# Expert 0's input rows are loaded and transposed inside the attention, into the memory of the low-rank projections

## The chip, the cores and the metric

The kernel runs on one core of a Trainium2 chip, as one launch. The metric is the device time of one execution in microseconds (us), median of several runs. Engines are named as in the profile: PE (TensorE, its weight loads as PEld), DVE (VectorE), ACT (ScalarE), POOL (GpSimd) and SP (SyncE, which only issues DMAs here).

## The reference

Two transformer blocks on 2 x 2048 tokens of width 256 in float32. Each adds an attention and a feed-forward of the same layernormed input to the residual.

```
x = L0_attn_x
xn = _layernorm(x, axis=-1)
x = x + _L0_attn_ref(xn, ...) + _L0_ffn_ref(xn, L0_ffn_Wg, L0_ffn_W_in, L0_ffn_W_out)
xn = _layernorm(x, axis=-1)
x = x + _L1_attn_ref(xn, L1_attn_key_param, ...) + _L1_ffn_ref(xn, ...)
return x
```

- Block 0's attention is causal with low-rank projections: `q = x @ Wqa @ Wqb` (rank 64), `kv = x @ Wkva @ Wkvb` (rank 32), 16 query heads of width 16 on 4 key heads, rotary embedding, softmax, output projection.
- Block 0's feed-forward is a mixture of 8 experts: each token goes to its two best experts, each expert has places for 1280 tokens, and computes `gelu(a) * g` from its 256 x 1024 input weights and then a 512 x 256 output product. The results are weighted with the gates and added.
- Block 1's attention is against 32 fixed pattern keys, with a sparsemax in place of the softmax. Its weights do not depend on the tokens, so that they can be folded together ahead (`Wq` with the keys, `Wv` with the keys).
- Block 1's feed-forward is a mixture of 8 experts with sigmoid scores, and a shared expert.

## The kernel before, in words

The kernel has three stages: block 0's attention (with the routing of its experts inside), block 0's experts, and block 1.

**Stage 1, attention (L274 to L1171).** Low-rank projections of all tokens are kept in `low` (L285, filled at L374). From it come queries and keys by the products of L385 to L390 and L432 to L436, through DRAM (`qd`, `kd`) back into the tiles `q` and `ks`. The 32 work items j (batch, block of 512 queries, group of heads) are handled in a fixed order. For each there are two passes: `maxima` (L454; scores `s` and their row maxima on DVE, L471), whose result is flipped on PE (`mtT`, L485), copied by DVE into `mr` (L490) and written into two rows of the query tile by DMA (`place_max`, L492), and then `score` (L500; scores `sc` on PE, exponentials `es` on ACT at L510, a mask on POOL at L512) and `values` (L515; `av` on PE). When four items of a block are done, `normalize` (L526) transposes `av` on DVE and `project` (L550) multiplies with the output weights into `po`, DVE adds it to `xo` (L556), and SP stores `xo` into `x1` (L558).

Meanwhile the routing is computed, and POOL scatters the normalised token rows, each with its target and gate (258 words), to the experts' places in the DRAM array `buf` (`dispatch`, L656, 64 indirect DMAs). Expert 0's weights are loaded late in this stage into `cs_sb` (`wi0`, `wt0`; L272, L1169), whose rotary tables are no longer needed by then.

The order of instructions in this stage is written by a loop (L1153) with a cost model: `T` holds a model time of each engine, `candidates()` (L1093) offers the next steps on PE with the time at which each could start, and the best one is written. Steps on other engines and DMAs are put into `jobs` by `later` and written by `flush` (L691) when the model says that they are ready. Instructions written by `pin` keep this order on their engine.

PSUM is shared in this stage by `ps2` (2 tiles of two banks: maxima, flips, projections), `pssc` (3 banks: scores) and `psav` (1 bank: `av`).

**Stage 2, experts (L1215 to L1308).** The memory of stage 1 is given back and given out again. Here the order on each engine is the scheduler's, which follows the program's data and its own estimates. ACT issues ten loads of block 1's weights that are to be folded (L1215 to L1228). Then, for each expert: SP loads its 1152 rows from `buf` (`load_rows`, L1236; 1161 KB), DVE takes targets and gates out of them (`places`, L1241), PE transposes the rows in 18 steps of 128x128, ACT and DVE copying the result into `inT` (`transposed`, L1248). Then come three blocks of 384 rows (`feed_forward`, L1260): for each of four parts, two products `pa` and two `pg` (L1267; each of 128 rows against 384 columns), a Gelu on ACT (L1269) and a product on DVE into `hT` (L1270); then three times four products `py` (L1274), a scaling by the gates on DVE into `ys` (L1277) and a scatter with addition to `x1` by POOL (L1279). Rows and weights of later experts are loaded by SP ahead, into two buffers each. A branch at L1300 handles experts with more than 1152 tokens.

**Stage 3, block 1 (L1310 on).** The weights are folded (L1352 to L1384), and the rest is written by a list scheduler (`Plan`, L49), whose instructions all carry line L138.

Of the kernel before, what the change touches and what calls it, by code (L numbers as in the profile page):

```python
# [145 lines left out]
def moe_transformer_kernel(  # L146
# [121 lines left out]
    cctx = ctx.enter_context(ExitStack())  # L268
    csp = cctx.enter_context(tc.tile_pool(name="csp", bufs=1, side="right"))
    cs_sb = csp.tile([P, 2, S], F32, name="cs_sb")  # L270

    wi0 = cs_sb[:, 0].rearrange("p (c f) -> p c f", c=2)  # L272
    wt0 = cs_sb[:, 1, 0:4 * E].rearrange("p (c e) -> p c e", c=4)
    with ExitStack() as actx:  # L274
# [7 lines left out]
        ps2 = actx.enter_context(tc.tile_pool(name="ps2", bufs=2, space=PSUM))  # L282
        pssc = actx.enter_context(tc.tile_pool(name="pssc", bufs=3, space=PSUM))
        psav = actx.enter_context(tc.tile_pool(name="psav", bufs=1, space=PSUM))
        low = attw.tile([96 + NE, NT], F32, name="low")  # L285
        wq16 = attw.tile([64, 2, 16, 16], F32, name="wq16")
        wkv16 = attw.tile([96, 12, 16], F32, name="wkv16")
        wout_sb = attw.tile([P, 2, E], F32, name="wout_sb")
# [80 lines left out]
        def lows(grp):  # L369

            ps = ps2.tile([P, 512], F32, tag="ps2", name="lw")
            for dc in range(2):
                mm(ps[:96 + NE], lhsT=wa_sb[:, dc], rhs=st[grp]["xnT"][:, dc], start=dc == 0, stop=dc == 1)
            pin(A.copy(low[:, 512 * grp:512 * grp + 512], ps[:96 + NE]))  # L374

        def logits(grp):
            tp = ps2.tile([P, 4, NE], F32, tag="ps2", name="tpl")
# [278 lines left out]
        def dispatch(ti, k):  # L656
# [2 lines left out]
            pin(G.indirect_dma_start(ways[(2 * ti + k) % 4], bass.IndirectOffsetOnAxis(ap=idx_sb[:, k, ti:ti + 1], axis=0),  # L659
                                     xss[ti], None, bounds_check=NSLOT - 1, oob_is_err=False))  # L660

# [428 lines left out]
        def candidates():  # L1093
            now = T["PE"]
            sw = lambda mode: SWITCH * (mode != model["mode"])
            if pos["sc"] < len(scs):
                t = scores_at(now)
                yield t - now + sw("sc") - (150 if T["A"] < now + 300 else 0), t, do_scores
            if pos["av"] < len(avq):
                j, c = avq[pos["av"]]  # L1100
                t = max(now, when("es", j, c, 0), when("es", j, c, 1), at.get("av", 0) if c == 0 else 0,
                        when("v", j // 16, c // 4))
                if c == nch(j) - 1 and j % 4 == 1 and at.get("atts", 0) == 2:
                    t = INF
                yield t - now + sw("av"), t, do_values
            if flips:
                t = max(now, when("neg", flips[0]), free2[-2])
                yield t - now + sw("f") - 400, t, do_flip
            if pos["u"] < len(units):
                j, i, kb = units[pos["u"]]  # L1110
                slack = (main_at[j] - model["scores"]) - (unit_end[j] - model["maxima"]) - LEAD
                t = max(now, when("q", j), when("k", j // 16, kb), free2[-2])
                t2 = max(t, free2[-1] - 230)
                late = -600 if slack < 1 else 0 if slack < MOST else 900
                yield t2 - now + sw("s") + late, t, do_maxima
            for k, (due, ready, dur, f) in enumerate(prep[:1]):
                t = max(now, ready(), free2[-2] if dur else 0)
                late = -500 if due - model["maxima"] < 2 else -100 if due - model["maxima"] < 9 else 2500
                yield t - now + late, t, lambda k=k: prep.pop(k)[3]()
            if projects:  # L1120
                bq, i0, ready = projects[0]
                t = max(now, ready, when("xo", bq), free2[-2])
                late = -300 if now > ready + 15000 else 100

                def go():
                    if i0:
                        projects.pop(0)
                    else:
                        projects[0][1] = 2
                    p_project(bq, i0)  # L1130
                yield t - now + late, t, go
# [18 lines left out]
        for i in range(NSLOT // 512):  # L1150
            later("S", ISSUE, 50000 + 12000 * i, lambda i=i: clear(buf, i), None, 2)
            later("S", ISSUE, 340000 + 40000 * i, lambda i=i: clear(buf1, i), None, 2)
        while pos["av"] < len(avq) or jobs or projects or scat["ti"] < NTILE:  # L1153
            prefetch()
            refetches()
            keys_back()
            scatter()
            flush()
            cand = [z for z in candidates() if z[1] < INF]

            events = [job[4] for job in jobs if job[4] > T["PE"]] + [T["S"], T["V"], T["G"], T["A"]]
            events = [t for t in events if t > T["PE"]]
            best = min(cand, key=lambda z: z[:2]) if cand else None
            if best and best[1] <= min(events + [INF]) + 400:
                best[2]()
            else:
                t1 = min(events) if events else T["PE"] + 500
                T["PE"] = t1
            if not prep and not at.get("w0") and pos["u"] > len(units) - 20:  # L1169
                at["w0"] = 1  # L1170
                later("S", 2 * ISSUE, T["PE"], lambda: load_expert(0, wi0, wt0), None, 2)  # L1171

    x_sb = ctx.enter_context(tc.tile_pool(name="xp", bufs=1)).tile([P, NTILE, E], F32, name="x_sb")
    l1w = ctx.enter_context(tc.tile_pool(name="l1w", bufs=1))
# [37 lines left out]
            v = v.rearrange("p (a b c) -> p a b c", a=shape[1], b=shape[2])  # L1212
        return v

    sq = {}  # L1215
    for nm, ap in (("wqT", wqT), ("wk", wk), ("wv", wv)):
        sq[nm] = fold_tile(P, 2, E)
        A.dma_start(sq[nm], ap.rearrange("(c p) m -> p c m", p=P))
    kp_sb = fold_tile(P, 2, NPAT)
    A.dma_start(kp_sb, kpT.rearrange("(c p) m -> p c m", p=P))  # L1220
    bqk = fold_tile(P, 2, 2)
    A.dma_start(bqk, bqk2)
    bv_sb = fold_tile(1, E)
    A.dma_start(bv_sb, bv)
    A.dma_start(wo_sb, wo.rearrange("(c p) m -> p c m", p=P))
    A.dma_start(bo_sb, bo.broadcast_to([P, E]))
    A.dma_start(gw_sb, gw.rearrange("(c p) m -> p c m", p=P))
    A.dma_start(lb_sb, lb)  # L1228


    with tc.tile_pool(name="moe", bufs=2) as mp, tc.tile_pool(name="moeh", bufs=3) as hp, \
            tc.tile_pool(name="moetp", bufs=2, space=PSUM) as mtp, \
            tc.tile_pool(name="moeps", bufs=2, space=PSUM) as mps:
        tiles = CAP0 // P

        def load_rows(e):  # L1236
            rows = mp.tile([P, tiles, ROW], F32, tag="rows", name="rows")
            SP.dma_start(rows, buf[CAP * e:CAP * e + CAP0].rearrange("(c p) d -> p c d", p=P))
            return rows

# [19 lines left out]
        def feed_forward(wi, wt, inT, n, to, gates_e, c0, x1s):  # L1260
            hT = mp.tile([P, 4, STEP], F32, tag="hT", name="hT")
            for f in range(4):
                pa = mps.tile([P, 512], F32, tag="pa", name="pa")
                pg = mps.tile([P, 512], F32, tag="pg", name="pg")
                for ps, col in ((pa, P * f), (pg, FF + P * f)):
                    for dc in range(2):
                        PE.matmul(ps[:, :n], lhsT=wi[:, dc, col:col + P], rhs=inT[:, dc], start=dc == 0, stop=dc == 1)  # L1267
                ge = hp.tile([P, STEP], F32, tag="ge", name="ge")
                A.activation(ge[:, :n], pa[:, :n], AF.Gelu)  # L1269
                V.tensor_tensor(hT[:, f, :n], ge[:, :n], pg[:, :n], ALU.mult)  # L1270
            for i in range(n // P):
                py = mps.tile([P, E], F32, tag="py", name="py")
                for f in range(4):
                    PE.matmul(py, lhsT=hT[:, f, P * i:P * i + P], rhs=wt[:, f], start=f == 0, stop=f == 3)  # L1274
                c = c0 + i
                ys = hp.tile([P, E], F32, tag="ys", bufs=6, name="ys")
                V.tensor_scalar(ys, py, gates_e[:, c:c + 1], None, ALU.mult)  # L1277

                G.indirect_dma_start(x1s[c % len(x1s)], bass.IndirectOffsetOnAxis(ap=to[:, c:c + 1], axis=0), ys, None,  # L1279
                                     compute_op=ALU.add)  # L1280

        STEP = 384
        last = bass_types.dram_disjoint_views(x1[:], 3)
        rows = load_rows(0)
        for e in range(NE):
            wi, wt = experts[e]
            to, gates_e = places(rows, tiles)
            inT = mp.tile([P, 2, CAP0], F32, tag="inT", name="inT")
            transposed(rows, tiles, inT)
            if e + 1 < NE:  # L1290
                rows = load_rows(e + 1)
            for c in range(2):
                SP.dma_start(wall[P * e:P * e + P, P * c:P * c + P], fg[:, c, e])
                SP.dma_start(wall[P * e:P * e + P, E + P * c:E + P * c + P], fu[:, c, e])
            SP.dma_start(wall[P * e:P * e + P, 2 * E:3 * E], fd[:, e])
            for s0 in range(0, CAP0, STEP):
                feed_forward(wi, wt, inT[:, :, s0:s0 + STEP], STEP, to, gates_e, s0 // P, last if e == NE - 1 else [x1[:]])
            if e + 2 < NE:
                experts.append(next_expert(e + 2))
        with tc.If(tc.nc.values_load(longer[0:1, 0:1], min_val=0, max_val=1) > 0):  # L1300
# [753 lines left out]
```

## Time and profile before

| what | value |
|---|---|
| runs: median, lowest, highest | 2124.32, 2123.40, 2124.34 us |
| the profiled execution's own time | 2125.51 us |
| its span, first to last instruction | 2123.8 us |
| mean granted TensorE clock | 0.952 of full speed |
| stage 1 ends on PE (last `po`) | about 1201 us |
| stage 2 ends on PE (last `py`) | about 1605 us |
| expert 0, PE, from first `tp` to expert 1's first `tp` | 1209.3 to 1262.4 us |
| DMA, mean | 89 GB/s |

Times in the profile are microseconds from the first instruction. A timeline row has the start, the length, the engine, the line, the operation, the tile written and the tiles read, shapes and a count; in brackets stands how long the engine was idle before, and what ended that wait. One matrix product in float32 makes two rows of PE where it needs two passes of weights, so that two products of `pa` appear as x4. The granted clock is the share of TensorE's full speed that the chip's throttle allowed in a stretch. A line such as L310 or L138 is that of a helper that writes many kinds of instruction: there the names of the tiles tell them apart.

### The profile page before, as it was taken

The page shows a single profiled execution, that of the slowest core. Times are in us where ns is not written, and L with a number is a line of the kernel's source. Part 1 is how long each engine was busy: PE and PEld are TensorE (multiplying, and loading weights), DVE is VectorE, ACT ScalarE, POOL GpSimd, SP SyncE. Part 2 cuts the span into 40 slices and gives each one's busy share as a digit, 9 for nine tenths or more (in the row PEclk, how much of TensorE's full clock was granted, in tenths as well). Part 3 has the DMA queues.
Part 4 walks back from the last instruction along what each step waited for, and adds up shares of the span by engine and source line. Part 5 has one row for each costly group of instructions (what it writes and reads, how often), then busy time and mean ns, then how long its engine had stood idle before and what let it go on. Part 6 is the DMA issues. An engine that isn't in the chain of part 4 may idle for free. (4 is left out here: it accounts for less than half of the span.)

```text
span 2123.8 us, 26286 instructions
## 1 busy us (share of the span) xinstructions
PE 1927.7 (91%) x9525; PEld 1070.7 (50%) x9534; DVE 1386.4 (65%) x1943; ACT 913.7 (43%) x1834; POOL 721.2 (34%) x914
## 2 busy tenths in 40 slices
PE   4689999899999999999999799999998998878886
PEld 2344443444444444444443366666765755666664
DVE  4576688676787578778784122222226599999896
ACT  3044456355555655665567411111112333554452
POOL 5232211443444333431101022222230088466551
PEclk8599899899999999999999899999999799999999
DMA  5433321242132322321200333333223022444417
GB/s 148 127 118 103 101 71 38 82 130 67 59 101 84 100 91 64 92 85 32 91 11 11 123 82 75 77 77 77 52 28 105 11 80 88 134 146 145 154 59 238
DMA packets 141384, 188.98 MB, mean 89 GB/s; under 512 B 15678, under 2 KB 109252, under 8 KB 141251
## 3 DMA queue, kind: packets, MB, share of 16 engines
q1 hardware_dynamic: 114672, 135.03, 21.1%
q0 software_dynamic: 23552, 50.46, 9.4%
q10 hardware_dynamic: 3026, 1.77, 0.3%
q8 instruction: 77, 1.26, 0.2%
q14 instruction: 57, 0.46, 0.1%
HBM read 100.74 MB, written 90.66 MB: 90 GB/s over the span
## 5 line engine op out<-in xcount | busy, mean ns | idle before, releaser
L510 ACT ACTIVATE es<-sc 128x512 f32<-128x512 f32 (+3 forms) x1280 | 599.6, 536 | 457.7 <-PE sc L310 447.0
L471 DVE TENSOR_REDUCE part<-s 128x2 f32<-128x1024 f32 (+3 forms) x640 | 650.4, 1059 | 210.5 <-PE s L310 209.3
L310 PE MATMUL sc<-q,ks 128*128 128x512 f32 (+3 forms) x1280 | 425.5, 418 | 19.5 <-ACT es L510 18.9
L310 PEld LDWEIGHTS sc<-q,ks 128*128 128x128 f32 x1280 | 211.7, 191 | 249.0 <-ACT es L510 174.5
L310 PE MATMUL av<-es,va 128*32 128x512 f32 (+3 forms) x2560 | 303.2, 552 | 3.4 <-POOL es L512 1.8
L512 POOL TENSOR_SCALAR_AFFINE_SELECT es<-es 128x256 f32<-128x256 f32 x256 | 103.4, 407 | 561.5 <-ACT es L510 560.5
L310 PE MATMUL s<-ks,q 64*128 64x512 f32 (+3 forms) x1280 | 253.1, 447 | 33.8 <-DVE part L471 11.2
L138 DVE TENSOR_TENSOR srt<-srt 128x1024 f32<-128x1024 f32 (+3 forms) x224 | 224.0, 1036 | 7.6 <-ACT to L138 0.5
L310 PEld LDWEIGHTS s<-ks,q 64*128 64x128 f32 x1280 | 111.6, 189 | 200.6 <-DVE part L471 110.5
L1279 POOL DMA_INDIRECT x<-ys,to x72 | 111.5, 1549 | 294.6 <-DVE ys L1277 165.5
L1270 DVE TENSOR_TENSOR hT<-ge,pg 128x384 f32<-128x384 f32 x96 | 53.2, 554 | 178.1 <-PE pg L1267 176.9
L1269 ACT ACTIVATE ge<-pa 128x384 f32<-128x384 f32 x96 | 47.1, 490 | 269.4 <-PE pa L1267 269.4
L138 POOL DMA_INDIRECT oe<-xn,to x80 | 109.3, 1367 | 76.0 <-ACT xn L138 56.2
L1267 PE MATMUL pa<-inT,wi 128*128 128x384 f32 x336 | 123.3, 486 | 0.0
L1267 PE MATMUL pg<-inT,wi 128*128 128x384 f32 x336 | 122.1, 486 | 0.0
L138 POOL DMA_INDIRECT buf<-xn,slot x64 | 87.7, 1371 | 99.9 <-DVE rc L138 80.7
L1274 PE MATMUL py<-wt,hT 128*128 128x256 f32 x504 | 112.2, 379 | 0.0
L138 ACT COPY srt<-srt 128x1024 f32<-128x1024 f32 (+2 forms) x80 | 67.2, 840 | 101.6 <-DVE srt L138 89.4
L310 PEld LDWEIGHTS av<-es,va 128*32 128x32 f32 x2560 | 55.7, 109 | 100.5 <-issue 76.3
L1274 PEld LDWEIGHTS py<-wt,hT 128*128 128x128 f32 x504 | 95.8, 190 | 17.5
L1277 DVE TENSOR_SCALAR ys<-py,gates 128x256 f32<-128x256 f32 x72 | 34.8, 484 | 86.0 <-PE py L1274 86.0
L1267 PEld LDWEIGHTS pg<-inT,wi 128*128 128x128 f32 x336 | 63.3, 190 | 42.7
(265 smaller groups left out, 2308.2 us busy)
## 6 DMA issues: line engine op xcount, KB each, us to landing
q<-qd SPq DMA_DIRECT2D x64, 256.0 KB
buf<-zero SPq DMA_DIRECT2D x20, 516.0 KB
buf<-zero SPq DMA_DIRECT2D x20, 514.0 KB
xn<-buf SPq DMA_DIRECT2D x20, 514.0 KB
rows<-buf SPq DMA_DIRECT2D x8, 1161.0 KB
qd<-hi SPq DMA_DIRECT2D x16, 512.0 KB
qd<-lo SPq DMA_DIRECT2D x16, 512.0 KB
xn<-oe SPq DMA_DIRECT2D x16, 512.0 KB
```

The lines of the kernel that those rows point to most:

```text
L138: return lambda *a, **k: self.tc.keep_in_program_order(f(*a, **k))
L310: pin(PE.matmul(*args, **kw))
L471: pin(V.tensor_reduce(parts[j][:, i, 2 * pair:2 * pair + 2, kb], sc[:, :, :n], AX.X, ALU.max))
L510: pin(A.activation(es[:, g % 2, :n], sc[:, :n], AF.Exp, scale=0.25))
L512: pin(G.affine_select(es[:, :, 0:P], es[:, :, 0:P], pattern=[[0, 2], [1, P]], compare_op=ALU.is_ge, fill=0.0, base=0, channel_multiplier=-1))
L1267: PE.matmul(ps[:, :n], lhsT=wi[:, dc, col:col + P], rhs=inT[:, dc], start=dc == 0, stop=dc == 1)
L1269: A.activation(ge[:, :n], pa[:, :n], AF.Gelu)
L1270: V.tensor_tensor(hT[:, f, :n], ge[:, :n], pg[:, :n], ALU.mult)
L1274: PE.matmul(py, lhsT=hT[:, f, P * i:P * i + P], rhs=wt[:, f], start=f == 0, stop=f == 3)
L1277: V.tensor_scalar(ys, py, gates_e[:, c:c + 1], None, ALU.mult)
L1279: G.indirect_dma_start(x1s[c % len(x1s)], bass.IndirectOffsetOnAxis(ap=to[:, c:c + 1], axis=0), ys, None, compute_op=ALU.add)
```

## The change

- `low` is allocated in the pool beside `cs_sb`, on 128 partitions, so that it outlives the attention. Its memory, when the projections are no longer needed, holds expert 0's rows (`rows0`) and two of three parts of its transposed rows (`inT0`); the third lies in the free half of `cs_sb`.
- When expert 0's weights have been asked for and all scatters are written, SP gets three loads of 384 rows each (`load_rows0`).
- When all maxima are written, the loop may write `turn_rows0`: six transposes on PE into one `ps2` tile and one copy of 128x768 on DVE, three times.
- In stage 2, expert 0 uses these; `rows` of even experts live in `rows0`, those of odd experts in one other buffer, where there were two.
- `py` gets a PSUM pool of its own, ahead of that of `pa` and `pg`. So `pa` and `pg` lie where the attention's `pssc` and `psav` were, and `py` where a part of `ps2` was.
- The ten loads of weights to be folded are issued by SP in the program's text of expert 1, not by ACT ahead of stage 2.

```
@@
-        low = attw.tile([96 + NE, NT], F32, name="low")
+    low = csp.tile([P, NT], F32, name="low")
+
+    rows0 = low[:, 0:CAP0 // P * ROW].rearrange("p (c d) -> p c d", d=ROW)
+    inT0 = [low[:, CAP0 // P * ROW + 768 * i:CAP0 // P * ROW + 768 * i + 768] for i in range(2)] + [cs_sb[:, 1, 4 * E:4 * E + 768]]
+    inT0 = [v.rearrange("p (c n) -> p c n", c=2) for v in inT0]
@@
+        def load_rows0(i):
+            sdma(rows0[:, 3 * i:3 * i + 3], buf[384 * i:384 * i + 384].rearrange("(c p) d -> p c d", p=P))
+
+        def turn_rows0(i):
+
+            tp = ps2.tile([P, 2, 512], F32, tag="ps2", name="tp0")
+            for dc in range(2):
+                for c in range(3):
+                    flip(tp[:, dc, P * c:P * c + P], rows0[:, 3 * i + c, P * dc:P * dc + P], ident)
+            pin(V.tensor_copy(inT0[i], tp[:, :, 0:384]))
@@ candidates()
+            if pos["u"] == len(units) and at.get("turned", 0) < 3:
+                i = at.get("turned", 0)
+                t = max(now, when("row0", i), free2[-2])
+
+                def turn():
+                    at["turned"] = i + 1
+                    t = use2(1500, "t", 0, lambda: turn_rows0(i))
+                    free2.append(on("V", 1000, t))
+                yield t - now + 200, t, turn
@@ the loop
+            if at.get("w0") and scat["ti"] == NTILE and not at.get("r0"):
+                at["r0"] = 1
+                for i in range(3):
+                    later("S", ISSUE, T["PE"] + 8000, lambda i=i: load_rows0(i),
+                          lambda t, i=i: at.update({("row0", i): t}), 2)
@@ stage 2
-        A.dma_start(sq[nm], ap.rearrange("(c p) m -> p c m", p=P))
...
+    def load_fold():
+        for v, ap in ((sq["wqT"], wqT), (sq["wk"], wk), (sq["wv"], wv), (kp_sb, kpT), (wo_sb, wo), (gw_sb, gw)):
+            SP.dma_start(v, ap.rearrange("(c p) m -> p c m", p=P))
+        SP.dma_start(bqk, bqk2)
+        SP.dma_start(bv_sb, bv)
+        SP.dma_start(bo_sb, bo.broadcast_to([P, E]))
+        SP.dma_start(lb_sb, lb)
@@
+            tc.tile_pool(name="moepy", bufs=2, space=PSUM) as mpy, \
             tc.tile_pool(name="moeps", bufs=2, space=PSUM) as mps:
@@
+        rows_of = [rows0, mp.tile([P, tiles, ROW], F32, tag="rows", bufs=1, name="rows")]
+
         def load_rows(e):
-            rows = mp.tile([P, tiles, ROW], F32, tag="rows", name="rows")
+            rows = rows_of[e % 2]
@@
-                py = mps.tile([P, E], F32, tag="py", name="py")
+                py = mpy.tile([P, E], F32, tag="py", name="py")
@@
-        rows = load_rows(0)
+        rows = rows0
...
             to, gates_e = places(rows, tiles)
-            inT = mp.tile([P, 2, CAP0], F32, tag="inT", name="inT")
-            transposed(rows, tiles, inT)
+            if e == 0:
+                parts_in = inT0
+            else:
+                inT = mp.tile([P, 2, CAP0], F32, tag="inT", name="inT")
+                transposed(rows, tiles, inT)
+                parts_in = [inT[:, :, s0:s0 + STEP] for s0 in range(0, CAP0, STEP)]
             if e + 1 < NE:
                 rows = load_rows(e + 1)
+            if e == 1:
+                load_fold()
```

More of the change, by code (lines that the diff above doesn't have):

```diff
@@ L373, in lows @@
                 mm(ps[:96 + NE], lhsT=wa_sb[:, dc], rhs=st[grp]["xnT"][:, dc], start=dc == 0, stop=dc == 1)
-            pin(A.copy(low[:, 512 * grp:512 * grp + 512], ps[:96 + NE]))
+            pin(A.copy(low[:96 + NE, 512 * grp:512 * grp + 512], ps[:96 + NE]))
         def logits(grp):
@@ L1152, in moe_transformer_kernel @@
             later("S", ISSUE, 340000 + 40000 * i, lambda i=i: clear(buf1, i), None, 2)
-        while pos["av"] < len(avq) or jobs or projects or scat["ti"] < NTILE:
+        while pos["av"] < len(avq) or jobs or projects or scat["ti"] < NTILE or at.get("turned", 0) < 3:
             prefetch()
@@ L1213, in fold_tile @@
         return v
-    sq = {}
-    for nm, ap in (("wqT", wqT), ("wk", wk), ("wv", wv)):
-        sq[nm] = fold_tile(P, 2, E)
-        A.dma_start(sq[nm], ap.rearrange("(c p) m -> p c m", p=P))
[L1219 to L1228, printed above, removed]
+    sq = {nm: fold_tile(P, 2, E) for nm in ("wqT", "wk", "wv")}
+    kp_sb, bqk, bv_sb = fold_tile(P, 2, NPAT), fold_tile(P, 2, 2), fold_tile(1, E)
+    def load_fold():
[5 more added lines that the diff above has]
+        SP.dma_start(lb_sb, lb)
     with tc.tile_pool(name="moe", bufs=2) as mp, tc.tile_pool(name="moeh", bufs=3) as hp, \
             tc.tile_pool(name="moetp", bufs=2, space=PSUM) as mtp, \
+            tc.tile_pool(name="moepy", bufs=2, space=PSUM) as mpy, \
             tc.tile_pool(name="moeps", bufs=2, space=PSUM) as mps:
         tiles = CAP0 // P
+        rows_of = [rows0, mp.tile([P, tiles, ROW], F32, tag="rows", bufs=1, name="rows")]
         def load_rows(e):
-            rows = mp.tile([P, tiles, ROW], F32, tag="rows", name="rows")
+            rows = rows_of[e % 2]
             SP.dma_start(rows, buf[CAP * e:CAP * e + CAP0].rearrange("(c p) d -> p c d", p=P))
@@ L1296, in moe_transformer_kernel @@
             for s0 in range(0, CAP0, STEP):
-                feed_forward(wi, wt, inT[:, :, s0:s0 + STEP], STEP, to, gates_e, s0 // P, last if e == NE - 1 else [x1[:]])
+                feed_forward(wi, wt, parts_in[s0 // STEP], STEP, to, gates_e, s0 // P, last if e == NE - 1 else [x1[:]])
             if e + 2 < NE:
```

## The prediction

> **What bounds the kernel now.** First the page's busy line and its slices: TensorE (PE) is busy nine tenths of the span, so a change gains where PE stands still or runs slowly.
>
> ```profile
> PE 1927.7 (91%) x9525; PEld 1070.7 (50%) x9534; DVE 1386.4 (65%) x1943; ACT 913.7 (43%) x1834; POOL 721.2 (34%) x914
> ...
> PE   4689999899999999999999799999998998878886
> ...
> PEclk8599899899999999999999899999999799999999
> ```
>
> Slice 23 (1168 to 1221 us) shows a 7 among nines. It is where the attention ends and the experts begin, the place that the change touches. The timeline of PE there:
>
> ```profile
> 1193.31 0.70 PE L310 MATMUL po<-wout_sb,att 128*128 128x256 f32 x2
> 1196.04 4.98 PE L310 MATMUL po<-wout_sb,att 128*128 128x256 f32 x14 [2.03 <-DVE att L541]
> 1209.30 1.94 PE L1254 MATMUL tp<-ident,rows 128*128 128x128 f32 x8 [8.29 <-DMA rows<-buf]
> ...
> 1231.36 1.45 PE L1267 MATMUL pa<-inT,cs_sb 128*128 128x384 f32 x4
> ...
> 1241.68 5.34 PE L1274 MATMUL py<-cs_sb,hT 128*128 128x256 f32 x24
> ...
> 1246.86 1.45 PE L1267 MATMUL pa<-inT,cs_sb 128*128 128x384 f32 x4
> ...
> 1262.36 1.04 PE L1254 MATMUL tp<-ident,rows 128*128 128x128 f32 x8
> ```
>
> PE ends the last projection (po) at 1201.02, waits 8.29 us for expert 0's rows, and only then transposes them. One block of 384 rows costs 15.5 us when nothing is missing (1231.36 to 1246.86); the first block takes from 1209.30 to 1231.36, 22.06 us. The table of stages gives the reason for much of that (columns: stretch, its length, busy us of PE, PEld, DVE, ACT, POOL with counts, granted clock, DMA share, GB/s):
>
> ```profile
> 1190.00:1193.00 3.00, 2.55 (x27) 1.23 (x24) 0.00 (x0) 1.91 (x8) 1.58 (x4) 1.00 0.00 0
> 1193.00:1196.00 3.00, 1.01 (x6) 0.41 (x6) 1.68 (x3) 0.00 (x0) 0.62 (x1) 1.00 0.00 0
> 1196.00:1198.50 2.50, 2.46 (x8) 2.08 (x9) 0.41 (x1) 0.00 (x0) 0.00 (x0) 0.70 0.00 0
> 1198.50:1201.00 2.50, 2.50 (x7) 1.64 (x6) 0.28 (x1) 0.00 (x0) 0.00 (x0) 0.62 0.00 0
> ...
> 1205.00:1209.00 4.00, 0.00 (x0) 0.00 (x0) 0.00 (x0) 0.00 (x0) 0.00 (x0) 0.50 1.04 331
> ...
> 1214.00:1216.00 2.00, 2.00 (x6) 0.98 (x5) 0.69 (x1) 0.27 (x1) 0.00 (x0) 0.50 1.07 354
> ...
> 1218.00:1222.00 4.00, 4.00 (x14) 2.29 (x13) 1.11 (x2) 1.14 (x3) 0.00 (x0) 1.00 1.05 391
> ```
>
> The granted clock is halved from about 1197, recovers briefly, and is 0.50 again until about 1217. From 1222 to the last expert PE is busy over 99% of each stretch at clock 1.00, so what is gained here arrives at the end of the experts, and what follows (chain of waits: sorts on DVE, projections) starts from there.
>
> **The change, part by part.**
>
> *Removed wait.* Expert 0's rows no longer load after the attention: 8.28 us (1201.02 to 1209.30). What is late next is the Gelu: its table load and first call wait for the last po, 1.28 + 0.49 us by the timeline, while PE has 3.9 us of products to do before it needs that buffer. So nothing shows there.
>
> *Removed serial transposes and slow clock.* First block 22.06 minus 15.50 = 6.56 us. The rest of expert 0, two blocks, is unchanged.
>
> *Moved product.* In the changed program's order, the first pa (2 products, 1.29 us by 1.29 us from one pa to the next pg in a full block) stands behind the first po. It waits only for the transpose of av on DVE, which ends at 1194.25, and po resumes at 1196.04: it fits. Gain 1.3 us.
>
> *Clock.* The seven remaining po products take 4.98 us at the lowered clock; at the 0.43 us that a py of the same width takes (5.2 us for 12) they would take 3.0 to 3.1. PE was busy a third of 1193 to 1196; with pa there it is about three quarters. TensorE: Matmul & The Clock Gate, Part 1, of the Trainium skill says that the clock is halved after an idle window of about 3.4 us and restored after a busy one. The trace halves it after a hole of only 2.03 us beside thin work, so a window need not be empty. By the page's wording the clock stays up once the hole is filled (gain 1.9); by the trace alone a fall is still possible (gain 0). I take 1.9, since 90% busy stretches just before hold 1.00, and keep 0 for the range.
>
> *Added in the attention: 18 transposes on PE, 3 copies on DVE.* They stand beside the last flip of maxima and in the next 7 us.
>
> ```profile
> 1146.28 0.60 PE L313 MATMUL mtT<-ident,mt 128*8 128x128 f32 x4 [0.54 <-DVE mt L483]
> ...
> 1147.62 1.34 SPq L316 DMA_DIRECT2D q<-mr  x2
> ...
> 1154.81 0.50 PE L310 MATMUL sc<-q,ks 128*128 128x512 f32 x1 [0.16 <-ACT es L510]
> ```
>
> Eight transposes take 1.04 us in the row of 1262.36, 0.13 each, so 18 cost 2.3 us. The same page, Part 4, speaks against the change: about 275 ns for one transpose in a kernel. The records here show 273 ns too, but they overlap; by the page's figure 18 would be 5.0 us. I take the row. Six stand where PE waited 0.54 us; the other twelve stand among diagonal scores, where PE waits 0.16 to 0.34 us for the exponentials. Cost 1.5 us, bounds 0.5 and 3. The DVE copies (128x768; a 128x512 one takes 0.68, so 1.0 us each by size) find DVE idle for 8.13 us, but the first is ahead of the copy of mr, which feeds the loads of the last maxima: these leave about 0.7 us later. They are issued at 1147.62 to 1148.96, and the scores that need them start at 1154.81, so over 2 us of cover remain with a landing of some 3 us; without it, 0.7 us.
>
> *Row loads, moved past SP's queue.* Three loads stand between the last q loads and the next mr loads:
>
> ```profile
> 941.07 2.57 SPq L316 DMA_DIRECT2D q<-qd  x4
> 960.04 1.45 SPq L316 DMA_DIRECT2D q<-mr  x2
> ```
>
> The first waits for the last scatter, which POOL issues at 947.23 (one lands about 5 us after the issue before it). So SP is held until about 952.5; behind it stands only the 960.04 load. 1161 KB at 331 to 400 GB/s take 3.5 us, done by 957. Cost zero; without that idle time up to 8 us of late maxima. PE needs the data at 1146.
>
> *Fold loads, moved from ACT's queue to SP's.* ACT loses ten issues that held nothing else. On SP they stand behind rows of experts 1 and 2 and the weights of experts 1 and 2. DMA: Bandwidth & Descriptors (Issuing engines are not separate DMA queues) says that the same 16 engines serve all issuers, so the bytes cost the same; the order does not. DVE, in order, now meets three waits on loads inside expert 0: rows 1 and rows 2 (for their slots), and bqk. All of these are late relative to the po end, 1200.6 in my sum. Rows 1, x1's store and rows 2 are 2834 KB: at 350 GB/s landed about 10 us after po. The first ys is due 11 us after it. bqk has about 7.1 MB up to it: 20.4 us plus 2 of latency gives 1223, and its issue waits for expert 2's weights to land, so up to 1226. DVE reaches that copy at 1223.1, with hT behind it that PE needs at 1226.4. I take 0.5 us for all these waits, bounds 0 and 3. Expert 1's weights (before bqk in the queue) are needed only at 1246. The buffers that moved in SBUF and PSUM add no instruction; I count zero.
>
> **The sum.** 8.28 + 6.56 + 1.3 = 16.1 (the same from the other side: 61.3 us from the po end to expert 1's first tp become three blocks of 15.5 less 1.3, 45.2); plus 1.9 for the clock, minus 1.5 and 0.5: 16.0 us. The profiled execution took 2125.51 us around its span of 2123.8, so 2109.5 for such a one; the median of the runs is 1.19 below it: 2124.32 - 16.0 = 2108.3.
>
> **The rivals.**
> *The sum without the clock, or with a dearer insertion (0.28).* The clock falls at the hole as before (+1.9), the insertion costs 3 (+1.5) or bqk arrives late (+2.5): 2109.8 to 2114.2, likeliest 2112. For it: the gate already fell in a stretch that was a third busy; against: the hole is filled.
> *Hidden anyway (0.04).* The experts' scatter-adds, not PE, set the end. On POOL's timeline they follow 4.5 us apart (1228.87, 1233.33); 72 of them are 324 us, from the first one (about 1214) to 1538, against 1600 for PE. It would give 2122 to 2126, with the gain left as idle PE at the end. Little speaks for it.
> *Slower (0.05).* DVE's queue in expert 0: bqk's copy blocks hT, and PE with it, until the load lands. Each us past 1226.4 costs one. The gain is eaten at 1242, and the time is slower by over 0.2% past 1247, which means 7.1 MB in 46 us, 155 GB/s. At 140 it would land at 1253, 27 us late: 2124.3 - 16.0 + 27 = 2135. The stretches above show 331 to 391.
> *The change does not do what it says* is left at almost nothing: in its order the row loads, transposes and copies do stand in the attention.
>
> **How the numbers follow.** My forecast 0.63 (2106.8 to 2109.8), the rivals 0.28, 0.04 and 0.05. The range runs from all bounds good (insertion 0.5, no waits: 2106.8) to the second case's end, 2114.2, and 0.9 us further at both ends, which is how far the three runs of before lie apart: 2105.9 to 2115.1. A measurement here tells about 0.2% (4.2 us) from no change: faster 0.91, same 0.04, slower 0.05.
>
> **What would show it.** In the new profile: no wait of PE for rows at the attention's end; the first pa inside the 2 us hole; granted clock near 1.00 from 1190 on; the first tp of expert 1 at about 1246; three row loads near 952 to 957; DVE's copy of bqk without a long wait; from expert 1 on, the same 48 us an expert. I am wrong if PE waits in expert 0 for hT or py for more than 3 us, if the last scores start over 2 us later, or if the experts' gain is lost before the end.

## The result, and the profile after

| | before | after |
|---|---|---|
| median of the runs, us | 2124.33 (2123.4 to 2124.51, 4 runs) | 2107.21 (2105.72 to 2109.07, 4 runs) |
| ratio to before | | 0.9914, 95% interval 0.9902 to 0.9927 |
| profiled execution, us | 2125.51 | 2105.72 |
| its span, us | 2123.8 | 2103.9 |

The change takes 17.1 us off the median; the interval of the ratio reaches from 15.5 to 20.8 us. The kernel was measured twice more beside the experiments, with ratios of 0.992 (0.9907 to 0.9934) and 0.9916 (0.9891 to 0.9941). The prediction was 16.0 us, a median of 2108.3 us.

The page of after, the rows of busy time, of PE's slices and of the granted clock:

```profile
PE 1922.6 (91%) x9534; PEld 1069.6 (51%) x9534; DVE 1387.5 (66%) x1943; ACT 912.4 (43%) x1831; POOL 716.0 (34%) x914
...
PE   4688999899999999999999999999998999888886
...
PEclk8599999899999999999999999999998799999999
```

The 7 and the 8 in the slice where the attention hands over to the experts (PE and clock) have become nines. PE's busy time is 5 us less, on as many matmuls (9534 records, 9525 before): the same work, less of it at a lowered clock. The timeline of PE over the same place:

```profile
1190.04 0.70 PE L313 MATMUL po<-wout_sb,att 128*128 128x256 f32 x2
1191.03 1.56 PE L1294 MATMUL pa<-low,cs_sb 128*128 128x384 f32 x4 [0.29 <-DVE t L536]
1192.77 3.29 PE L313 MATMUL po<-wout_sb,att 128*128 128x256 f32 x14 [0.18 <-DVE att L544]
1195.89 1.46 PE L1294 MATMUL pg<-low,cs_sb 128*128 128x384 f32 x4
...
1241.14 1.04 PE L1281 MATMUL tp<-ident,rows 128*128 128x128 f32 x8
...
1242.91 0.81 PE L1294 MATMUL pa<-inT,wi 128*128 128x384 f32 x2
```

Three things are to be seen. The wait of 8.29 us for rows is gone, and so are the transposes behind it: pg follows po at once. The first pa stands between the two po. From the start of the first po to that of the second it is 2.73 us, to the hundredth what it was before (1193.31 to 1196.04), so the product cost nothing there. And the seven po behind the hole (the 2 us between the two po) take 3.29 us, where they took 4.98. ACT starts its table load for the Gelu right behind the last po:

```profile
1196.13 1.28 ACT L1296 ACT_TABLE_LOAD   x1 [7.01 <-PE po L313]
```

The stages (stretch, its length, busy us of PE, PEld, DVE, ACT and POOL, granted clock, DMA share, GB/s):

```profile
1190.00:1193.00 3.00, 2.53 (x10) 1.21 (x8) 1.68 (x3) 0.00 (x0) 0.62 (x1) 1.00 0.00 0
1193.00:1196.00 3.00, 3.00 (x15) 2.64 (x15) 0.69 (x1) 0.00 (x0) 0.00 (x0) 1.00 0.00 0
1196.00:1200.00 4.00, 4.00 (x14) 2.35 (x13) 1.49 (x4) 2.27 (x3) 0.40 (x2) 1.00 0.71 188
1200.00:1210.00 10.00, 10.00 (x40) 7.30 (x39) 2.96 (x9) 0.98 (x2) 1.63 (x1) 1.00 1.05 362
```

PE is full from 1193 on at a granted clock of 1.00. The loads of the other experts' rows and weights keep the DMA engines as busy as before (1.05), now beneath PE's work.

**Where the time came from.** A single execution wanders by several us, so the stretch is measured between marks next to the change. M is the issue of the last but one pair of `q<-mr` loads of the attention (the expectations below call it the last maxima loads; the very last pair, at 1147.62 before, follows 45.3 us later, in after 45.7), P the first of the last po products, X the first pa of expert 1.

| us | M | M to P | M to X | span |
|---|---|---|---|---|
| before | 1102.36 | 90.95 | 161.76 | 2123.8 |
| after | 1098.47 | 91.57 | 144.44 | 2103.9 |
| after, second profile (c1_after) | 1094.94 | 91.55 | 144.43 | 2101.2 |
| after, third profile (c2_after) | 1099.67 | 91.61 | 144.47 | 2105.2 |
| e2_fold_only | 1098.69 | 90.93 | 158.76 | 2119.1 |
| e3_late_turn | 1096.64 | 91.02 | 150.45 | 2109.9 |
| e4_psum_back | 1103.30 | 91.61 | 148.51 | 2113.3 |
| e5_double_turn | 1094.97 | 93.47 | 146.34 | 2102.3 |
| e6_fill_hole | 1100.87 | 91.58 | 146.78 | 2110.6 |

From M to X the change gains 17.3 us. It divides into -0.62 up to P, 1.69 in the po (4.98 to 3.29), and 16.25 from po's end to X (1201.02 to 1264.12 before; 1196.06 to 1242.91 after). The three profiles of after agree within 0.04 us there, while M itself lies anywhere in 4.7 us. The profiled spans differ by 19.9 us: 3.9 of that had arisen before M, and after the experts 1.3 is lost again, which one profile of before can't put down to the change. Nor can the 3.9 be: e2_fold_only, with the attention of before, has M at 1098.69, and e4_psum_back, with that of after, at 1103.30.

### The profile page after: what moved, and what is told of

The parts are those of the page before. It is cut to its first block, busy times and chain, and to the rows that moved or that the text cites. A ratio compares the mean times of both kernels' runs of the same rounds, so it can differ in the third digit from the quotient of the medians.

```text
span 2103.9 us, 26294 instructions
## 1 busy us (share of the span) xinstructions
PE 1922.6 (91%) x9534; PEld 1069.6 (51%) x9534; DVE 1387.5 (66%) x1943; ACT 912.4 (43%) x1831; POOL 716.0 (34%) x914
## 5 line engine op out<-in xcount | busy, mean ns | idle before, releaser
L138 POOL DMA_INDIRECT buf<-xn,slot x64 | 83.1, 1299 | 100.8 <-DVE rc L138 81.6
```

Source lines behind the costliest of these rows:

```text
L138: return lambda *a, **k: self.tc.keep_in_program_order(f(*a, **k))
```

## The experiments

Each ratio is to the kernel before, measured beside the run. The median of before was 2126.32 us beside e1 to e4, 2124.79 beside e5, e6 and c1_after, and 2125.74 beside e7, e8 and c2_after, so ratios compare better than medians do.

**The fold loads put back on ACT (e1_fold_act).** Expert 0's rows stay in the attention; the ten loads are issued by ACT ahead of expert 0, as before.

```
     def load_fold():
-            SP.dma_start(v, ap.rearrange("(c p) m -> p c m", p=P))
+            A.dma_start(v, ap.rearrange("(c p) m -> p c m", p=P))
...
+    load_fold()
...
-            if e == 1:
-                load_fold()
```

> The changed kernel with its ten fold loads issued by ACT ahead of the experts, as before the change. My theory (the gain is expert 0's removed wait, its transposes and the clock; moving the fold loads is needed because ACT's queue would hold the Gelu): in the profile of before the ten issues took ACT from 1201 to 1211, so the first Gelu comes about 10 us after the last po in place of 1.5, PE stands about 8 us in expert 0, and the time is about 8 us above the changed kernel (some 2115). Rival (where the fold loads are issued does not matter, only the bytes do): within 1 us of the changed kernel, no PE wait in expert 0.

Measured: 2118.6 us, ratio 0.9961 (0.9948 to 0.9973): by the ratios some 9 to 10 us slower than after (8 were expected). The timeline of ACT and PE in this kernel (lines of other engines left out):

```profile
1198.58 0.46 ACTq L1248 DMA_DIRECT2D xn<-in_wqT_dram  x1
...
1201.45 0.48 ACTq L1248 DMA_DIRECT2D gw_sb<-in_gw_dram  x1
1204.03 0.35 ACTq L1249 DMA_DIRECT2D xn<-in_bqk_dram  x1
1207.42 0.49 ACTq L1250 DMA_DIRECT2D xn<-in_bv_dram  x1
1207.54 1.94 PE L1282 MATMUL tp<-ident,rows 128*128 128x128 f32 x8 [5.12 <-DMA rows<-buf]
...
1208.36 0.74 ACTq L1252 DMA_DIRECT2D lb_sb<-in_lb_dram  x1
1209.49 1.28 ACT L1297 ACT_TABLE_LOAD   x1 [17.89 <-PE tp L1282]
1210.79 0.87 ACT L1297 ACTIVATE ge<-pa 128x384 f32<-128x384 f32 x2
...
1211.33 2.93 PE L1295 MATMUL pa<-low,cs_sb 128*128 128x384 f32 x4
```

Ten issues ask for some 5 us of ACT but occupy it from 1198.58 to 1209.10, because up to 3 us pass between one and the next; what they wait for, the trace does not say. Only then come the table load and the first Gelu: the table load lies 108.5 us behind M, 10.9 us later than in the changed kernel (97.7, its row is shown above). PE has two pairs of pa and pg as cover, goes over to expert 1's transposes, waits 5.12 us for their rows, and then runs at a lowered clock (pa 2.93 us instead of 1.45). Measured from M to the start of the last py of the experts it is 489.58 us, against 480.01 in after and 497.34 before. Without the moved loads the rest of the change gains 7.8 us instead of 17.3.

**The fold loads moved alone (e2_fold_only).** The kernel before, with nothing but `load_fold` on SP in expert 1's text; rows, transposes and PSUM pools as before.

```
-        A.dma_start(sq[nm], ap.rearrange("(c p) m -> p c m", p=P))
+            if e == 1:
+                load_fold()
```

> The kernel before with only its fold loads moved to SP beside expert 1. My theory: rows of expert 0 land 1 to 3 us sooner for lack of company (8.3 us of PE wait become 6 to 7), transposes and slow clock stay: 2121 to 2123. Rival (the fold loads' traffic ahead of the rows was the cause of the wait, and moving them is most of the gain): the wait falls under 3 us and the time by 6 us or more, 2118 or less.

Measured: 2124.36 us, ratio 0.9983 (0.9975 to 0.9991); from M to X 3.0 us less than before. PE in this kernel:

```profile
1192.34 4.98 PE L310 MATMUL po<-wout_sb,att 128*128 128x256 f32 x14 [2.02 <-DVE att L541]
1204.30 3.84 PE L1250 MATMUL tp<-ident,rows 128*128 128x128 f32 x16 [6.98 <-DMA rows<-buf]
```

The wait for rows falls from 8.29 to 6.98 us; the likely reason, which no run separates, is that the ten loads no longer run beside those of the rows. The other 1.7 us lie in the first block. ACT before, and then here:

```profile
1201.05 0.46 ACTq L1218 DMA_DIRECT2D xn<-in_wqT_dram  x1
...
1210.55 0.34 ACTq L1228 DMA_DIRECT2D lb_sb<-in_lb_dram  x1
1211.32 0.58 ACT L1256 COPY inT<-tp 128x512 f32<-128x512 f32 x1 [18.94 <-DMA wo_sb<-in_wo_dram]
```

```profile
1205.46 0.59 ACT L1252 COPY inT<-tp 128x512 f32<-128x512 f32 x1 [16.77 <-PE tp L1250]
```

Before, ACT was still issuing until 1210.89, and its first copy of transposed rows began 2.02 us behind the first transpose (1211.32); here it begins 1.16 us behind it, and sixteen transposes follow each other. So the moved loads are worth 3.0 us where the rows come late, and 9.6 us where they are there.

**The rows loaded early, turned late (e3_late_turn).** As after, but the transposes are done in stage 2; the loads stay in the attention.

```
-            if pos["u"] == len(units) and at.get("turned", 0) < 3:
...
-            if e == 0:
-                parts_in = inT0
-            else:
...
+            inT = mp.tile([P, 2, CAP0], F32, tag="inT", name="inT")
+            transposed(rows, tiles, inT)
```

> The changed kernel with the rows loaded in the attention, but transposed only in expert 0, after the last po. My theory: the load wait is gone (8.3 us of gain stay), but 18 serial transposes (2.3 us at full clock, more at half), their copies in between (about 1 us), the pa that no longer fits the hole (1.3) and the clock that falls in the empty hole (1.9) come back, less 0.6 for the insertion: 6 to 9 us above the changed kernel, 2113 to 2116. Rival (the wait alone was the gain; the clock recovers as soon as there is no wait): 2 to 3 us above it, granted clock 1.00 in the transposes.

Measured: 2116.26 us, ratio 0.9948 (0.9927 to 0.997); from M to X 6.0 us more than after. PE in this kernel:

```profile
1190.39 4.97 PE L313 MATMUL po<-wout_sb,att 128*128 128x256 f32 x14 [2.02 <-DVE att L544]
1196.14 1.09 PE L1272 MATMUL tp<-ident,low 128*128 128x128 f32 x8 [0.78 <-DVE xo L559]
1197.52 0.66 PE L1272 MATMUL tp<-ident,low 128*128 128x128 f32 x4 [0.28 <-ACT inT L1274]
```

The rows are there, and PE still does not go on at once: nothing can stand in the hole, so the po run at a lowered clock (4.97 us, at 0.64 to 0.72 in stretches of 2.5 to 3 us), the first transpose waits 0.78 us for the last xo, and 18 transposes with their copies stand in PE's way. The loads in the attention cost nothing: M to P is 91.02, against 90.95 before. The 0.55 us that after has more (91.57) are the price of the inserted transposes.

**PSUM as before (e4_psum_back).** As after, with `py` in one pool with `pa` and `pg` again.

```
-            tc.tile_pool(name="moepy", bufs=2, space=PSUM) as mpy, \
...
-                py = mpy.tile([P, E], F32, tag="py", name="py")
+                py = mps.tile([P, E], F32, tag="py", name="py")
```

> The changed kernel with py back in the PSUM pool of pa and pg, so that no pa can run in the hole before the last po. My theory: the 2 us hole is empty again, the granted clock falls to about half in the last po products (about 5 us in place of 3.3), and the pa is paid after them: 3 to 4 us above the changed kernel. Rival (the clock has nothing to do with the hole, the two profiles differ there by chance): 1.3 us above it, clock 1.00 in the po products.

Measured: 2115.57 us, ratio 0.9952 (0.9936 to 0.9969); from M to X 4.1 us more than after. `pa` now lies in a buffer that xo still reads, so it can't go into the hole:

```profile
1194.91 0.70 PE L313 MATMUL po<-wout_sb,att 128*128 128x256 f32 x2
1197.63 4.97 PE L313 MATMUL po<-wout_sb,att 128*128 128x256 f32 x14 [2.02 <-DVE att L544]
1203.39 1.56 PE L1293 MATMUL pa<-low,cs_sb 128*128 128x384 f32 x4 [0.78 <-DVE xo L559]
```

The choice of a pool, which adds no instruction, is worth 4.1 us: 1.7 for the clock, 1.3 for the product in the hole, 0.8 for the wait, and 0.3 that no row names.

**The hole filled with products of no use (e6_fill_hole).** The one above, with two 512-wide products in the hole.

```
+                    if bq == 7 and (i0, i, u) == (0, 0, 0):
+                        fill = pssc.tile([P, 512], F32, tag="sc", name="fill")
+                        for _ in range(2):
+                            mm(fill, lhsT=ident, rhs=wout_sb.rearrange("p c e -> p (c e)"), start=True, stop=True)
```

> As e4 (py shares its PSUM buffers with the projections again, so the first pa comes only behind the last xo, and the hole between the two po is open), but with two 512-wide products of no use to the result in the hole. They take about 0.86 us together by the scores' rate, inside a hole of some 2 us. Theory (the clock falls because PE stands thin over the hole, and holds when the hole is filled): the po after the hole take 3.3 us instead of 4.97 at a granted clock of 1.00, and the profile is 1.2 to 2.0 us shorter than e4 between the last maxima loads and the first full set of pa of expert 1, which leaves 2.1 to 2.9 us over the changed kernel: the moved pa and a wait for xo. Rival (the clock falls for another reason, the length of the load before or the kind of product): po again 4.9 to 5.0 us, and no gain over e4, or a loss of up to 0.9 us if the products push the po back.

Measured: from M to X 146.78 us, 1.7 less than e4_psum_back and 2.3 more than after; the median, 2112.24 us, has a ratio of 0.9936 (0.9922 to 0.995) and is too coarse for it. PE in this kernel:

```profile
1192.98 1.88 PE L313 MATMUL fill<-wout_sb,ident 128*128 128x512 f32 x4
1195.17 3.29 PE L313 MATMUL po<-wout_sb,att 128*128 128x256 f32 x14 [0.30 <-DVE att L544]
1199.24 1.56 PE L1297 MATMUL pa<-low,cs_sb 128*128 128x384 f32 x4 [0.78 <-DVE xo L563]
```

The stages of e4_psum_back over the hole and behind it (columns as above):

```profile
1194.00:1197.00 3.00, 1.46 (x16) 0.59 (x10) 1.10 (x3) 0.00 (x0) 1.03 (x2) 1.00 0.02 5
1197.00:1200.00 3.00, 2.37 (x6) 1.92 (x7) 0.58 (x1) 0.00 (x0) 0.00 (x0) 0.62 0.00 0
```

And those of the kernel with the filled hole:

```profile
1191.00:1194.00 3.00, 2.85 (x22) 1.57 (x23) 0.97 (x2) 0.45 (x2) 1.15 (x4) 1.00 0.02 5
1194.00:1197.00 3.00, 2.70 (x12) 1.66 (x10) 0.94 (x2) 0.00 (x0) 0.37 (x1) 1.00 0.00 0
1197.00:1200.00 3.00, 2.22 (x10) 1.45 (x9) 1.39 (x4) 0.00 (x0) 0.40 (x2) 1.00 0.10 13
```

The same po, with the same inputs behind the same hole, take 3.29 instead of 4.97 us, because PE had something to do until just before. The products took 1.88 us, all of it in the hole: twice what was expected of them (0.86, which counted one pass for each where the record shows two) and still free. So it is the filled hole that keeps the clock in this place, whichever wide product fills it: `pa` does it in after, the products of no use do it here. In the four profiles with an open hole (before, e2, e3, e4) the po take 4.97 or 4.98 us, in all eight with a filled one 3.29.

**Every transpose twice (e5_double_turn).** As after, with 18 transposes more in the attention.

```
-            for dc in range(2):
+            for dc in [0, 1] * 2:
```

> Every transpose of the first expert's rows in the attention is done twice (18 transposes more on PE, nothing else). Theory (18 transposes cost what the issue of the groups shows, 2.5 us of PE, and part of it lies in PE's waits for the exponentials): 0.6 to 2.3 us more than the changed kernel, nearly all of it between the last maxima loads and the first po. Rival A (the transposes lie wholly in waits): at most 0.5 us more. Rival B (each costs its full record of about 273 ns): 4.9 us more.

Measured: from M to X 1.90 us more than after, all of it before P (93.47 against 91.57); the median, 2107.98 us, with a ratio of 0.9926 (0.9906 to 0.9947), can't tell. A group of six in the changed kernel, from its timeline of PE:

```profile
1141.69 0.82 PE L316 MATMUL tp<-ident,low 128*128 128x128 f32 x6
1142.40 0.60 PE L316 MATMUL mtT<-ident,mt 128*8 128x128 f32 x4
```

And the group of twelve in this one:

```profile
1138.21 1.47 PE L316 MATMUL tp<-ident,low 128*128 128x128 f32 x12
1139.52 0.60 PE L316 MATMUL mtT<-ident,mt 128*8 128x128 f32 x4
```

Six more cost 0.65 us, 0.11 each; three groups 1.95, and 1.90 arrive. The second set finds no cover at all, whereas the first set, of the same length, cost 0.55 to 0.62. PE's waits there hid about 1.4 us, among them the 0.54 for mt, and are used up. The figure of 275 ns that the prediction weighed against the row (the Trainium skill, TensorE: Matmul & The Clock Gate, Part 4) would have made 5.0 us of them; the row was right for transposes in a row.

**The changed kernel again (c1_after, c2_after).**

> The changed kernel once more, unaltered, as the yardstick for the two beside it. Theory (the gain lies between the last maxima and the first transpose of expert 1, 17.3 us of it, and everything else is the spread of one profiled execution): 16 to 18 us under the kernel before in the median, and the stretch from the issue of the last maxima loads to the first full set of pa of expert 1 again 144 to 145 us. Rival (the 3.1 us that the first profile gained near 205 to 245 us, ahead of everything that was changed, belong to the change): they are there again, and the median is 19 to 20 us under.

> The changed kernel unaltered, as the yardstick of the two beside it: 16 to 18 us under the kernel before, 2104 to 2110 us.

Measured: 2106.98 us (2102.95 to 2111.22, 6 runs) and 2106.79 us (2106.13 to 2112.05, 4 runs). By the medians that is 17.8 and 19.0 us under the kernel before beside them, by the ratios 17.0 and 17.9; the intervals of the ratios (14.0 to 19.8 and 12.5 to 23.2 us) are too wide to separate 16 to 18 from the rival's 19 to 20. The profiles can: M to X is the same as in the first one, M is not. What the first profile gained ahead of M is less than the 4.7 us by which executions of this one kernel differ, and e2_fold_only shows nearly the same gain with the attention of before.

**Wide products among the thin ones of the router.** If a filled hole keeps the clock, a stage further on should gain too: from 1610 to 1660 the changed kernel stands at a granted clock of 0.50 to 0.83, with PE busy 93% of the time or more. One such product ahead of each of the eight groups of logits (e7_warm_logits), and two (e8_warm_twice):

```
                 st["lg"] = psum("po")
+                pPE.matmul(st["lg"][:, 64:512], lhsT=ident, rhs=wo_sb.rearrange("p c e -> p (c e)")[:, 0:448], start=True, stop=True)
```

> The changed kernel, and one product of 448 columns of no use to the result ahead of each of the eight groups of router logits of the second layer (128x8 products that keep PE busy but thin; the profile of the changed kernel has a granted clock of 0.50 to 0.67 from 1610 to 1660 there). Theory (the clock falls where products are thin, and wide ones in between hold it, as the filled hole did): a group of 8 transposes and 16 logits takes 3.1 instead of 5.4 us at full clock, the added product 0.8: some 7 groups gain 1.5 us each, 5 to 10 us under the changed kernel. Rival A (one product a group is too little): the clock stays at a half, and the added products cost 1.6 us each, 8 to 13 us over the changed kernel. Rival B (what follows the router waits for other engines): PE is earlier there and the end stays within 2 us.

> As the one before, with two such products ahead of each group. Theory: clock 1.00 through the router, 16 products cost 12 to 13 us at 0.8 us, the gain is 15 to 16 us: 2 to 4 us under the changed kernel. Rival A (the clock stays at a half even so): 16 to 25 us over it. Rival B (other engines set what follows): within 2 us.

Measured: 2105.84 us, ratio 0.9905 (0.9886 to 0.9923), and 2106.12 us, ratio 0.9906 (0.9879 to 0.9933): not to be told from the changed kernel, so the forecast 2 to 4 us of the second are neither shown nor excluded. From the start of the last py to the end of the span it is 525.4 us in after (526.3 and 525.5 in its other two profiles), 526.8 with one product, 523.2 with two. Groups in the changed kernel, from the timeline of PE:

```profile
1637.42 1.95 PE L138 MATMUL tp<-ident,xn 128*128 128x128 f32 x8
1639.16 3.42 PE L138 MATMUL po<-gw_sb,xT 128*128 128x8 f32 x16
```

And with two products in each:

```profile
1641.56 1.07 PE L138 MATMUL tp<-ident,xn 128*128 128x128 f32 x8
1642.47 1.67 PE L138 MATMUL po<-wo_sb,ident 128*128 128x448 f32 x4
1643.98 1.85 PE L138 MATMUL po<-gw_sb,xT 128*128 128x8 f32 x16
```

The same 10 us of that stage in the changed kernel, with one product and with two:

```profile
1640.00:1650.00 10.00, 9.55 (x47) 9.46 (x46) 0.38 (x2) 3.67 (x7) 0.00 (x0) 0.50 0.00 0
```

```profile
1640.00:1650.00 10.00, 10.00 (x48) 8.58 (x46) 0.19 (x1) 3.72 (x7) 0.00 (x0) 0.59 0.00 0
```

```profile
1640.00:1650.00 10.00, 10.00 (x73) 8.51 (x73) 0.49 (x4) 3.62 (x7) 0.00 (x0) 1.00 0.00 0
```

With two, the clock holds at 1.00 in most of that stage, and a group takes 4.1 us in place of 5.0; with one it is between 0.50 and 0.59 from 1620 to 1650, so neither the theory nor rival A holds for that: the first two and the last two groups had most of it at full clock, the four between them at half. The 2.2 us that the pair shows in one profile are within what executions differ by. No version better than the changed kernel is shown.

## Why the prediction was right, point by point

- **The removed wait and the first block (8.28 + 6.56, and 1.3 for the moved product: 16.1).** Right: 16.25 from po's end to X. All three blocks of expert 0 pass without a wait of PE, and expert 1's first tp comes 45.1 us after po's end (45.2 forecast). The split was not as told, though: 1.3 of the 8.28 and 1.7 of the 6.56 us were put down to the rows, the transposes and the clock, and are won by moving the fold loads alone (e2_fold_only; next point).
- **"ACT loses ten issues that held nothing else."** Wrong; that the sum did not suffer was luck, since the change moves these loads anyway. The profile of before had it, in the rows shown under e2_fold_only, which puts it at 3.0 us alone. Above all the cover was not named: the wait for rows hid those ten issues, and with the rows early they cost 9.6 us (e1_fold_act). Alone the two parts gain 3.0 and 7.8 us; of the 17.3 that they gain together, 6.6 exist only with both.
- **The hole: pa fits, gain 1.3, clock 1.9.** Right. The po began 2.73 us after the first po, as before, and took 1.69 us less. That the filled hole did it is shown by e6_fill_hole (1.68 us from it alone). That it is the clock fits the size: in before, 2.5 us at 0.70 and 2.5 us at 0.62 are 1.7 us less than at full clock.
- **Insertion 1.5, bounds 0.5 and 3.** High: 0.55 to 0.62. The rate was near (0.13 us a transpose taken, 0.11 found), the waits hid more of it than was counted: behind M the first six push mtT from 43.92 to 43.93 us, so they cost nothing, and the other twelve make up the cost. The last maxima's loads left 0.4 us later (0.7 supposed), and no scores waited for them.
- **Waits of DVE in expert 0, 0.5, bounds 0 and 3.** Zero. The timeline of DVE has the three waits that were named:

```profile
1202.45 0.17 DVE L1270 CAST to<-rows 128x9 int32<-128x9 f32 x1 [1.86 <-DMA rows<-buf]
...
1207.18 0.17 DVE L1270 CAST to<-low 128x9 int32<-128x9 f32 x1 [1.42 <-DMA low<-buf]
...
1219.64 0.29 DVE L1402 COPY xn<-xn 128x256 f32<-128x256 f32 x1 [0.95 <-DMA xn<-in_bqk_dram]
1220.73 0.56 DVE L1297 TENSOR_TENSOR hT<-ge,pg 128x384 f32<-128x384 f32 x1 [0.79 <-PE pg L1294]
```

  Each is longer than nothing, and behind each DVE waits for PE again, not PE for DVE. The copy of bqk began 23.6 us after po's end; the forecast had 22.5 to 25.4.
- **Row loads on SP: zero.** Right. SP issued them at 945.75, after 6.0 us of waiting behind the q loads (8.9 were supposed), and the next load of mr left at 956.19 without being held.
- **The rivals.** The sum without the clock fell: its mechanism is real (e4_psum_back), but the filled hole keeps it away. *Hidden anyway* and *slower* fell with the first profile: the lead at X is there at the last py (480.01 us from M, against 497.34), and bqk landed in time.
- **The terms together:** the two costs were 2.0 us in the forecast and 0.6 in the profile, which is nearly all of what separates 16.0 from 17.3.

## What to carry to other kernels

Before an issue or a load is called free, name the wait that covers it, and price it for the case that the change takes that wait away: here the same ten issues went from 3.0 to 9.6 us. The hole of 2 us in TensorE's work cost its own length and then 1.7 us in the products behind it, so independent work placed in it paid back twice (1.3 and 1.7 us), and it took no more than another buffer to let it in. Measure a change of 1% between marks next to it in several traces: here these agreed within 0.04 us, while the starts of that stretch lay 4.7 us apart.

## What the runs showed of the hardware

- The clock fell without a long idle stretch. A hole of 2.0 us, in 3 us in which PE was busy for 1.0 to 1.5, was followed by a granted clock of 0.50 to 0.72 (before, e2, e3, e4); with 2.53 (after) or 2.22 to 2.85 (e6) of 3.00 busy it stayed at 1.00. Where between 1.5 and 2.2 it turns was not measured.
- Busy is not the same as full. In the router PE was busy 93 to 100% of the time with 128x8 products and transposes, at a granted clock of 0.50 (after and c2_after); two 448-wide products in each group brought it to 1.00 in most of that stage (e8), one did not (e7).
- DMA issues stood as a queue in front of ACT's other work: ten of 0.35 to 0.74 us held it for 10.5 us (e1_fold_act).
